# Another written order of the first and last graphs in a four-layer graph network on one core

## The chip, the core and the metric

The kernel runs on one core of a Trainium2 chip. The metric is the device time of one execution in microseconds (us). Before the change, three runs gave 2754.33, 2758.63 and 2764.74 us, so the median is 2758.63 us.

## The reference

There are 32 graphs of 512 nodes with 256 features, each with a dense 512 x 512 adjacency `adj`. Every graph goes through four layers, and every layer is `x = layernorm(x + layer(x))`, all in float32:

```python
# layer 0: GIN           h = (1 + eps) * x + adj @ x;  relu(h @ W1 + b1) @ W2 + b2
# layer 1: GAT, 4 heads  softmax over adj > 0.5 of leaky_relu(e_dst + e_src), times x @ W, plus bias
# layer 2: 8 heads       softmax(q k^T / sqrt(32) + log(adj + 1e-6)) v, then Wo and bo
# layer 3:               softmax((x W x^T) * adj, masked by node) x
```

Graphs do not depend on each other, so the work of several graphs can be interleaved freely.

## The kernel before, in words

`fast_path` first describes the work and then emits it. `prepare()` (weights, bounds) and `graph(g)` for each of the 32 graphs register steps with `plan.step`: a name, an engine, a duration that the planner assumes, the steps it comes after, the buffers it takes, and a function that emits its instructions. There are 11118 steps, 2077 of them matmul steps on PE. `Plan.run` then reads one long list, `ORDER` (a compressed text, decoded in `Plan.sequence`), and emits the steps one by one in just that order. Each engine executes its instructions in the order in which it got them, so `ORDER` is the schedule. What comes out of `Plan.run` besides is only which of several equal buffers a step takes.

```python
data = zlib.decompress(base64.b85decode(text))
...
for g, name in self.sequence(text):
    s = self.steps[g][name]
    ...
    s.emit()
```

The stock of buffers is small and sets how many graphs can be in work: 13 large ones (`B`, 128 x 2048 float32), 12 of half that size (`C`), 10 strips (`D`), 8 PSUM banks (`p`), at most 6 graphs alive.

Steps that the text below speaks of, with the graph's number ahead of the name where it matters (26i0 is step `i0` of graph 26; `P` is preparation):

- Layer 0: `la` loads the adjacency in four transfers of 256 KB with packets of 128 bytes (line 806), `lx` loads x with 512 packets of 1 KB (line 818), `at` and `atd` turn and complete it on DVE, then matmuls `h0`, `h1` (adjacency times x), `f0` to `f3`, `y0`, `y1`.
- Layer 1: `xt1`, `v10` to `v13`, then `Rt`. From `Rt` goes a round trip through DRAM that this text calls the R trip: `Rsi` stores 16 rows of 512 bytes (line 1030), `Rli` loads them back, broadcast to 128 partitions, as 1 MB (line 1037), ACT makes `z00` to `z33` of them (line 1089), DVE `zm` (line 1100), and the matmuls `o100`, `o110`, `o101`, `o111` (line 1122) use them. Then `d1`, `dt`, `yt`.
- Layer 2: `xt2`, `q`, `k`, `v2`, scores `s0` to `s7` (line 1278), exponentials on ACT (line 1291), a product on DVE (line 1300), attention `n0` to `n7` (line 1336). The softmax denominators are added up by DMAs on the POOL queue that add one SBUF buffer into another (`cd1` to `cd7` and `fd0`, `fd1`, lines 1311 and 1364). These are the sums that the change's rule speaks of: 1 MB each, packets of 8 KB. A `B` buffer that a sum reads comes free only when the sum has landed. The bias additions `xd1` to `xd3` (line 610) are DMAs of the same kind on the same queue. Then `d2` and the projections `p0`, `p1`.
- Layer 3: the result is normalised (`r30` to `r33` on ACT) and, for graphs 2 to 28, transposed by way of DRAM: `xw3i` stores it (line 695), `xl30i` to `xl33i` load it back in four transfers with packets of 128 bytes (line 708, 1024 packets each), and DVE finishes the transposition with `xe30`, `xe31` (line 727). Then the matmuls `i0`, `i1` (which need `xe3`), `t0` to `t3`, `w0` to `w3`, the last normalisation, and `out`.

SP issues all loads and stores, POOL all sums and bias additions, in the order of the list; an issue that has to wait holds up what stands behind it on the same engine. A matmul step of mode "any" runs as four 32-column parts or as one whole, according to the step before it; changing between these modes costs PE about 0.1 us.

Of the list, the middle is periodic: one graph's worth of steps of several graphs, interleaved, repeats every 83 us. Only the start (where the first graphs fill the pipe) and the end (where the last ones drain) are irregular.

Of the kernel before, what the change touches and what calls it, by code (L numbers as in the profile page):

```python
# [37 lines left out]


ORDER = (  # L40
    'c-rk;*^=bA4Fo}ux~uw{@%D}<?En8tBNL#idcEV=h<$Q|)H78&cp-6+Dx@SLCAZiUY;jy-Po=2(Kg9|4bIQx=--7b0qlKcZttiWH'
    ')UVi3wM1o+(N!sO?!@kSboLOnRjaZznpU2Y$`ZAfigFx>7Bf_=cD7N9##YpPD_$7~C|;ijj(UEXt@>3xHy;76N3rVlOPui!^;)B1'
    'Ze~6<@4HqL?@k{BpjaHe4@7HgrzkZB5`)A)G;N7_%hThlvR`h%*6Krqs$-zO7j<HsYzpl{fE;>AQ!w0m*00uTE2l8Ejf-A4WNBW2'
    '4MJq#X=SuP5JH6P#V`c+U=X@h%2q=WQG{DGQ3DOr?6X2uJYkwxL1k7$g_Vt?mKP{STpw^dE>;>3pc5T!q^Ja=mN0cfntHDR6-}+u'
    'nAw>=j45i>kgBHehK2<CjV1-9U<=_7rvXvZ8qx+z1{47&mBZEmQM3)%hf9v}c)M=zYHS5n6Q(Fnd<EK~4WKa&-#CIwtMEFK7{TzX'
    'p3qbXlF&YFUbSH)=?-kNp&5Ewbe=<S%;9PD$dqkZcJ2{<3sX+_hDA^m<M{mmmU5a0J8Z25=0@P9VJi?by7t06RU56#iy5^PaRg;h'
    'GeisdYJgaVh$S>b^Rn|)sQh6(3}7(?$T2Kf#z<w1Q#sPg0Og(pQ>8j62%3Od8l5dHDV6+i$d+EAh<`A9wm6hRkpe&jO64G2EtP(m'
    '8wZM^hA*bYmNYelfl3SEfZ3RL=!KflI2=QV)Au8+0o1~8|MI?JI_#{mE5x-C)lzpxZ*3INOQj;!LqWQviyxIEmN7<I3E^4@;u>x2'
    'Apms=TZo7c_=f?`5N~X1_Ap<AUHEbHCdE#WT{zcZ4b8!=>OdFB16mA+P1B7c=qW8PK*+wrXd)`){F0y0Tn)<-j8dL-BaX8vBk?)X'
    'CwqScyl9Mr8G&B{CkxwpY9Q=Y($P*)O&Fu9o)Muw1+a6@ezs%I5*6@1$`2J}Oy_jY*q&pz)MR#_A^xcaD<kwjnn~xvF|R63B(@BA'  # L50
    'Et*Dv$TKo#K&%ah{umasoc;>gazXn`XrGrp7ql0&S3tO+y`a6Iy<+VJ?FH=x?FH=x?FH?%Lb$B<g7$*;3J90gUeI39UeNxZLp!kj'
    'HMGp+Cb&%9NVcJW6WqT5ZK5}zwXfLzDYW*C?K3b5?Z_CX=p)}0=x1&X*{&ya?a@kkK>J5zllPHXb9|M|f%@1@42GGYR^S(TJ3vFS'
    'gm8~3GbG1kWYM%_ww6WfnK&K?nMT$$D;PgB&zZx+2NL|k%zlaT7;5IPp=eS9*mDpO+y=6PNDx{b8F>lorRJHjEX;~psI!h_xIL1f'
    'gQ8)CLn6bCTw$U0F{_xMG$v6a4=p2A3pR*>J;Nk6c_oE=HT<A*uLOmlW^2r;m(xrNE%x-SikvO`X+fSa=44x<m}$*OWoPDnWV4xO'
    'rXsXiQ=Fp=8oUK*k>jt7JCAH<&;o)H!*0BKWwJha0>vJw?MUtNvjHm6u#@6_fn*`T<D?c<ij^a@;05SOABY`46+lJ?`jKNDJ3#>o'
    'PKBPFof`6!fiw&k))n-L<dk4|O53*6w>?bAA2<{aQh2q7hf6SSf-@seA>d?-aOlBG0HdM~Z8AWC6VQTt60wdH9VY6NlH-#_8<Ip^'
    'Am;<(P<^ct`zG)Y39VQQEjrTL+8{QyWTk*okz6E1Y{%LQSwO1^q&=Vm!9?rB2K7PQ3By8L4Ky4wLO}RoqCROCtq{<Y?qosAAR7!#'
    'wV2~X2UF%G1u5h6X-;x-r0O6nJZnbU7e$$zWFc?{nkHw)P8wE5^FT2e4uhBi{)1^N5mGdQEj<k^H8Rx7@K4Mo3S-U?fMK-MHd+cV'
    '0UwKiLAf=(_hIV1lA<P$WE4V#X~_VAbC*yeSa=L1G&CD?bV&|PP@956!Hr6$PeC~~nMKe>b_Tl0=?|t4buqq?l43Pt6y2*?ix@fh'
    'UKwUi?uhD;ffOnwQ6ktTUnW%yMbeGgIs*?md58~SuW(wSl8WUuGF=$qp2Ic2O0iUXFpzZUi@GP%NFO{Zx)zNo)<_z@NLh8nuMymz'  # L60
    'uEh*$BTxs551F5tWlt*#D>(`2=}S*cks!u>xsdbKFm<cJ71L0J=`)+kNV1DL?qs!CdD2H!J^3!DcQa5Eu0c1-s^mW9e3=;VVoV!='
    '`AdbgB28-GSi?OQEa&3o!E3TX9IJu%SoTGe^e;PEI-&T{^yu%Y_3?f7KPZ0BOQWykoLHXyA<F+^8~5(=^70~^TP9p7*|s|Zn)O*~'
    '@8ZrORF?0z`rE&HndhYceOAP=36slUrg_mH|Nen?dhat?wI-W4b^}?k%Cz~J*CNLuNp(D;twV0xA$3O(srYgLUdt{<2Gazls@Ya!'
    'vW1Mx!d1so%H}hPY#Ro`722|FvhJ_bzAww$y1z&;A>H#_ggN$SHYMfdwk*s1rjxX7*-P1dh|{rcL8xOG*j&728jMsfLH%kYfyydp'
    ')mZHYO_|MC&W5q$AIA~vWrucO?+&*^l6NTQ>ePPrzAQgcwEN-a=(<z)*|cl>&GkKdG@Yi-MiomgF5O&nb8MJiK_}ya4Ae0nS}ZFt'
    'FP+P`bJ^qyVo$z5&s}ZjI&-PLF+@#PkJ>qOTUU<p_WgUEFpGTKNG!!1KFNgU=G)|ooF>-+{`JWRR2s47^yU*b_9pvLxo~t1%v@b^'
    '{n3H}yK%A>TD(Wmvbg43=j>o_Z*N|`LxqlsnWHg7Fi?U8En>AN6PlW^xh(&5$aT^=S$vJ>g8}X>4kPw~c!AkPpZYvQVO?HQCz2#$'
    'u6k|XcO1Vm-mZ+Mj$t=DjwR&m(5AcfauZvyJ8t9-xA$rFzY36e!-nOe*Pco{?Gs(jK(o8<=t8~_C|v4cwc3IN9H4$m-rIbBVzy=g'
    '2mZmfZSE3SpZS6d8lIO79<Hp`K?s#L^nf)0mfV0mjM!FL*Y)PQSV5|Voh&Nv-fwp;AXH2atHWgR3*dqE4DX|2+qn9yk{s{V!Sb!F'
    ';_+Z!mQuI2NSR?%Q&yTnt{HbS7LkrX)_t$jw`n0+Uu>!#tUO{JsF1|w!~a|dO_s3lnFgL-K*b4%io?a~&95#uU~D%~V_oHRk`U*H'  # L70
    'avjmgg^o2gZd2S*`ebofVI6S;=;2+Gyd6&^+$+4$73CU{@B9&>!z>ZJaK8gd=MKuJx|_MuK2(B=84nV0sFVuUO5GP2iA(CrpCUXT'
    'htllOoCOH(0t5_ee2{<%PLRSK&ENf8`y@D@9#uTJdNZ5WwJzTCBKPlJ`gViv-``d49+Tad%iRY7QE{Vuw{}buZiv3?#`{p=ZMnL4'
    'nnzF#-YXwwU|?_ym~PXwo6+MuSSzAIU-=LO@6d&ebW9<LU_n)-1;TYabOASSy3e?iS-gn_igllGjN(337!Lz}cu{e?Yz{D%hP)SR'
    '?m`|H_*@0b-AbV2H5;d`gZ08l;)xBfyU`=#gBI>GWP3QEcBBjgq(7dvB0;3~X~buw`tc#+&J;Hxkk@N;rKaFBh(bT$b+>P~+wJY`'
    '<6eSY??L9Zn#Tr}m)=*d;2p<0VWQvPxon3MV@h#k{P4}AY2SPj<ZVj)h(QZ@&tK^|H^-2DCeiP6JW0{sq^<V!Bfie_QrpU(m2e-;'
    'Cq&%sSHgfPQR3$isxD$y87m6TsT%kHyva4P(@V@UK{ggSpUSCYVEn<uBT@;RF$Fvx*@<7AQiyO4+`Am{^PV4nljOjEb9<pG@HPLy'
    '-Nk<+D;KoCgqFz41?>gx6%a0HFK91luULCQdqI0adqI0adqI1x5H72|puM2I0>Wjr7ql0&7qtK9(DpA>i2n)g6S#mEp9^wQe-GTh'
    '0Ik>;Xv<e@{}ftz#`XzXTExUR&Zri7Y$vvoL|+BC@{H~iy!H(37i7;jL-A!jkLH84z}M)M;+Xzp168gvE$st)Asa%G+5<17%O3hf'
    '%S%~jauXYk!Nl?Y{deThe)BH*TC4gbNqblfa{H~y{mzu#3ymgT=*Bd?%oYNi$@d}wN)wP$!2bP^$krWYyyfa0rEK@Xztp5E3#hpX'
    '6o?K%q>BtTSTuf;>D+u7QYD`_Xvg3>v~{qBnL`8#HEs4J*h?@e08+e_4xAEVy6+JYHqubHBI|hbkOa@6%rDs9nNGL&U>oXjl(eMa'  # L80
    'eTv-tug;>&0=5ei#4U)=Ose1K*=7YZ0K=bYEH2rq(rLf27Law*^8#z|GD=%poBPC3Pe=swZB=1hw<^ccigsOkDIc9Lc$<ptYcY~F'
    'KuTUIC|_}8i{R)ETO;&+DNMHGMQ%*ZN-~#PyJZ^P5gOV>#<)<gk4FR|NzQj4(R7&Dr8<Kz4!R&x<rK1h_}`n<R}hSE#WA~)uzvSH'
    '2YlBXPV9~#e2Bn%ESvWZlAP#DmLJT4<i|2B75p4H*ZqEP%>julv&fNl{Gkps^4PB{2fnVff_)ialavc+cam24_9<9r$IHCdW!uO;'
    '0Oi9S0;Hy1U7sFs$gzb(gRN25btP%rCM%$xfb1Y`3ZfGg5(I^&GQ58T&%Via-vC#zp4=|hSJjyu6mR%AmSd5!%p)M9m+)NV*f*xt'
    '%c_!3I#kX(jGEH=gcom-D-}T{JdXjvzOb*7RK_<k+IVlIkWE8^+RvY)1_15PPY>>U-L}e5-TLZ-nA>FG=ZusxO+L(Cl*AzLF_Kv5'
    'k^R>CQJKt73ZKLi7<^`c4^R{hmXE?Qx3U&!ZY}woNLhmOF^l7HxIItW+5(GPmgduTBSRAtgind{TzW0tx~pyuhD&V>Fz5&LDh$k>'
    '!-Aq3!JI_n7TzPl*1>T32T(vNnl<<gGpVcR{5SgrGPGQBVi%|3c1xFDdRZsBm?)`y;WeOu)tFwve~1W29u&BDV9UCZHkik%3$FB+'
    '7gUf<Q92aq1^Ys_G1(Wve+JbSd>}Bpx_0o>R!7=BppkfMKjE&+E5!V#n^f!hdO|*>BQ;);sBm6Cmun-56#zIIyzHWOpP=142nB-P'
    'yo0!+ZG9=OC@(RinEL-|_Fy}$n6{>%+aSg*HoM(fom-no@z621y88HTOH#hwL){)o0G08!$__5&H=ifo`fKesyS;go_RWKcuOnu#'
    '(Aqk=*MK6{z<?*AjqgVkkRQR8fn*a2quqm&#}gT=7kT5fccT&bMZbEx?LLz2=6c)Q;|bHg3@;jSbMrH6UG!Yyb;OEkt}ZYpKOnkp'  # L90
# [1991 lines left out]
```

## Time and profile before

| | |
|---|---|
| median of three runs | 2758.63 us |
| the profiled execution's own time | 2757.91 us |
| its span, first to last instruction | 2756.2 us |
| PE busy | 2699.6 us (98%) |
| DVE, ACT, POOL busy | 2162.4 (78%), 1716.5 (62%), 480.4 us (17%) |
| mean granted TensorE clock | 0.992 |
| DMA queue q0 (POOL: sums, bias additions) | 45568 packets, 277.89 MB, 53.4% of the 16 engines' time |
| DMA queue q1 (SP: loads and stores) | 429872 packets, 136.18 MB, 24.4% |
| a sum on the POOL queue, issue to landing | min 6.9, median 8.8, max 17.3 us |

The span is what the engines did; the execution's own time is 1.7 us longer. PE's busy time counts matmuls that overlap by some 0.17 us at their ends as one. "Idle before, releaser" names how long an engine stood still ahead of an instruction and whose end set it free. The granted clock is the share of full speed at which TensorE ran.

### The profile page before, as it was taken

The numbers are of one execution on the slowest core, as the hardware profiler recorded it, in microseconds if no ns is written. First come the engines' busy times: TensorE is split into PE (matmuls) and PEld (weight loads), VectorE is DVE, ScalarE is ACT, GpSimd is POOL, SyncE is SP. The second block draws the span as 40 slices with busy tenths as digits, with TensorE's granted clock in tenths as the row PEclk, the third lists the DMA queues.
The fourth block names the chain that finished last, engine by engine and source line by source line (L and its number), as shares of the span: only waits on it lengthen the run. The fifth ranks groups of instructions, "written<-read, shape, count | busy, mean of one in ns | idle before, by whom it ended". The sixth has DMA issues, their size and how long they took to land.

```text
span 2756.2 us, 68553 instructions
## 1 busy us (share of the span) xinstructions
PE 2699.6 (98%) x28884; PEld 1309.0 (47%) x28884; DVE 2162.4 (78%) x4257; ACT 1716.5 (62%) x3320; POOL 480.4 (17%) x526
## 2 busy tenths in 40 slices
PE   8999999999999999999999999999999999898998
...
GB/s 169 81 137 148 162 164 163 170 158 162 168 155 152 173 161 162 159 158 154 169 161 170 155 154 158 176 159 170 147 160 149 175 154 159 153 93 150 152 127 33
DMA packets 476739, 418.80 MB, mean 152 GB/s; under 512 B 377789, under 2 KB 431497, under 8 KB 444553
## 3 DMA queue, kind: packets, MB, share of 16 engines
q0 software_dynamic: 45568, 277.89, 53.4%
q1 hardware_dynamic: 429872, 136.18, 24.4%
...
## 4 chain that ended last, share of the span: by engine, by line
PE 81%; DMA 4%; DVE 3%; issue 1%; ACT 1%; SPq 1%; POOL 0%; DVEq 0%; POOLq 0%; ACTq 0%
PE s L1278 8%; PE o_ps L1336 7%; PE o_ps L331 7%; PE o_ps L1122 6%; PE v_ps L331 6%; PE hT_ps L331 6%; PE y_ps L327 5%; PE h1T_ps L331 4%; PE s L331 4%; PE o2p_ps L331 4%; PE s L327 3%; PE iT_ps L327 3%; DMA z<-z 2%; PE qT_ps L327 2%; PE kT_ps L331 2%; PE kT_ps L327 2%
## 5 line engine op out<-in xcount | busy, mean ns | idle before, releaser
L1300 DVE SCALAR_TENSOR_TENSOR z<-AT,z 128x1024 f32<-128x1024 f32 x512 | 609.5, 1214 | 97.6 <-ACT z L1291 97.0
L1291 ACT ACTIVATE z<-s 128x512 f32<-128x512 f32 x1024 | 540.0, 607 | 141.3 <-PE s L1278 129.8
L1089 ACT ACTIVATE z<-R_bc,nT,S 128x512 f32<-128x512 f32 x512 | 374.6, 807 | 89.6 <-DMA z<-z 77.6
L669 ACT ACTIVATE x<-x,shift,rstd 128x256 f32<-128x256 f32 x508 | 273.8, 594 | 174.1 <-DVE shift L654 164.3
L1100 DVE SCALAR_TENSOR_TENSOR z<-z,T,edge 128x512 f32<-128x512 f32 x512 | 347.7, 744 | 16.5 <-ACT z L1089 16.4
L646 POOL TENSOR_TENSOR rstd<-ve,nhalf 128x4 f32<-128x4 f32 (+1 forms) x131 | 173.2, 1371 | 897.2 <-DVE ve L640 885.7
L1311 POOL DMA_DIRECT2D z<-z x186 | 174.8, 943 | 874.4 <-PE o_ps L1336 481.8
L1278 PE MATMUL s<-qT,kT 32*128 32x512 f32 x2048 | 272.8, 626 | 6.5 <-ACT kT L1249 6.5
L1336 PE MATMUL o_ps<-z,v 128*32 128x512 f32 x2048 | 249.7, 596 | 0.0
L1524 DVE TENSOR_TENSOR z<-s,AT 128x512 f32<-128x512 f32 x128 | 88.0, 690 | 204.1 <-PE s L327 104.0
L1150 DVE TENSOR_TENSOR z<-z 128x512 f32<-128x512 f32 (+1 forms) x256 | 229.5, 950 | 6.0 <-PE o_ps L1122 5.4
L1122 PE MATMUL o_ps<-z,v 128*32 128x512 f32 x2048 | 229.4, 593 | 1.1 <-ACT z L1291 1.1
L623 DVE BATCH_NORM_STATS2 st<-x 128x6 f32<-128x256 f32 x508 | 212.8, 419 | 11.0
L331 PE MATMUL o_ps<-x,z 128*32 128x257 f32 x3744 | 214.3, 380 | 0.0
L331 PE MATMUL hT_ps<-AT,x 128*32 128x384 f32 (+2 forms) x2592 | 181.5, 383 | 0.0
L327 PE MATMUL y_ps<-w_sb,h1T 128*128 128x256 f32 x816 | 180.9, 379 | 0.0
L1278 PEld LDWEIGHTS s<-qT,kT 32*128 32x128 f32 x2048 | 96.6, 184 | 142.0 <-issue 52.8
L331 PEld LDWEIGHTS o_ps<-x,z 128*32 128x32 f32 x3744 | 120.9, 110 | 87.8 <-issue 5.7
L327 PEld LDWEIGHTS y_ps<-w_sb,h1T 128*128 128x128 f32 x816 | 152.9, 190 | 19.6
L331 PE MATMUL h1T_ps<-hT,w_sb 128*32 128x512 f32 x1312 | 147.2, 592 | 0.0
L610 POOL DMA_DIRECT2D x<-biases x96 | 107.2, 1139 | 177.5 <-issue 72.5
L1122 PEld LDWEIGHTS o_ps<-z,v 128*32 128x32 f32 x2048 | 65.3, 110 | 149.3 <-issue 125.3
...
## 6 DMA issues: line engine op xcount, KB each, us to landing
...
```

Source lines behind the costliest of these rows:

```text
L327: nc.tensor.matmul(out, lhsT, rhs, start=start, stop=stop)
L331: nc.tensor.matmul(out[part], lhsT[:, part], rhs, start=start, stop=stop)
L623: nc.vector.bn_stats(t[f"st{n}"][:, c, :], t["xo" if n == 4 else "x"][:, c, :D])
L669: nc.scalar.activation(t[into][:, c, :D] if into else xn, xn, AF.Identity, bias=t[f"shift{n}"][:, c : c + 1], scale=t[f"rstd{n}"][:, c : c ...
L1089: nc.scalar.activation(t[f"e{h}"][:, c, :], t["Rbc"][:, h, :], AF.Relu, bias=t["nT"][:, h, c : c + 1], scale=t["S"][:, h, c : c + 1],)
L1100: nc.vector.scalar_tensor_tensor(z, z, t["T"][:, h, c : c + 1], t["edge"][:, c, :], op0=ALU.add, op1=ALU.mult)
L1122: nc.tensor.matmul(po[32 * q : 32 * q + 32, :], t["v"][:, c, hp * P + 32 * q : hp * P + 32 * q + 32], t[f"e{2*hp+q//2}"][:, c, :], start=( ...
L1150: nc.vector.tensor_add(z[:, :m, :], z[:, :m, :], z[:, m : 2 * m, :])
L1278: nc.tensor.matmul(pk, t["k"][hs, o, blk(c)], t["q"][hs, o, :], start=True, stop=True)
L1291: nc.scalar.activation(t[f"E{k}"][:, j, :], t[f"ps{k}{j}"], AF.Exp, scale=QSCALE)
L1300: nc.vector.scalar_tensor_tensor(z, t["AT"][:, c, None, :].to_broadcast([P, 2, N]), ADJ_EPS, z, op0=ALU.add, op1=ALU.mult,)
L1336: nc.tensor.matmul(t[f"n{o}"][32 * j : 32 * j + 32, :], t["v2"][:, c, o * P + F2 * j : o * P + F2 * (j + 1)], t[f"E{k}"][:, j, :], start=( ...
```

## The change

Only the text `ORDER` changes. The same 11118 steps are emitted, in another order; no step is added, removed or altered, and the rule by which the order was searched is not in the kernel.

```diff
 ORDER = (
-    'c-rk;*^=bA4Fo}ux~uw{@%D}<?En8tBNL#idcEV=h<$Q|)H78&cp-6+Dx@SLCAZiUY;jy-Po=2(Kg9|4bIQx=--7b0qlKcZttiWH'
...
-    'RB#@ZF;SgQu^J<aoNJ@=9kgSg4{Lm_^w<{i`Pi}B-h__gO@8qb+3-gB4`D>{SO'
+    'c-rk;?Q-Kd4g?91)TbTW$;@PD=N{wU|IrTJAZ6!j?`o^|*WF4pacqeq!NwOAw3(70B9h`5Z)6-P9ar)={2flDjB{w@=TwDnRW;5@'
...
+    'I{M^0IXch0omW)*h0#1~mLZ0sY5YP<H0|U2TOZFy^6~r<B}mE4*ehD5_;|>SJ`%6<6Hizkt+mS&O>^?On5mkd&}bDee#P5o74O^p'
 )
```

Decoded, the two lists compare so. Of the 2077 matmul steps, the places 7 to 386 and 1661 to 2056 differ; the 1274 between (from the middle of graph 6 to graph 25; 508 to 2167 us in the profile of before) and the last 21 are the same. The changes of matmul mode fall from 497 to 487.

As an example, matmul steps (PE) and the issues on POOL between 26p1, the last matmul before the DRAM transposition of graph 26, and 26i0, the first matmul after it:

```text
before  PE    26p1 27s6 27n3 27n4 28y1 27n5 27s7 29h0 29h1 27n6 29f0 28xt10 28xt11 29f1 28v10
              28v11 28v12 28v13 29f2 28Rt 29f3 26i0
        POOL  27cd1 27cd3 26dev3 27cd5 27cd2 28dev1 25dev4 27cd7 27fd0 27cd6 29xd1
after   PE    26p1 29h0 29h1 27n1 27s7 28xt10 28xt11 29f0 27n2 27n3 28v10 28v11 29f1 29f2 29f3
              27n4 27n5 27n6 28v12 28v13 26i0
        POOL  28dev1 27cd1 27xd3 26dev3 29xd1 27cd3 27cd5 25dev4 27cd7 27cd2
```

Only the order on one engine binds; how PE's list and POOL's interlock is settled by what each issue waits for. A sum `cd` of an odd number k waits for `n` of k - 1 and for its own product, 29xd1 for 29h1, and each waits for the issue ahead of it on POOL.

At more places the matmul steps between two dependent ones change: between 29Rt and 31h0 there stand more (31h0 moves back, behind 29o100 and 27w3), between `Rt` and `o100` of graphs 0, 1, 2, 5, 28 and 29 fewer, and graph 28's `p1` and `i0` stand closer together. At the start, SP issues the four adjacency strips of graph 0 ahead of its x (before: x second), ACT issues `eps` first (before: the two attention vectors first), and PE transposes two weights between 0h1 and 0f0 (before: behind 0y1).

More of the change, by code (lines that the diff above doesn't have):

```diff
@@ L40 @@
 ORDER = (
-    'c-rk;*^=bA4Fo}ux~uw{@%D}<?En8tBNL#idcEV=h<$Q|)H78&cp-6+Dx@SLCAZiUY;jy-Po=2(Kg9|4bIQx=--7b0qlKcZttiWH'
[L42 to L90, printed above, removed]
@@ L91 @@
-    'n<FvLQ_NyhFb!iO^C-55W%=OJjy!B{TZ1>8kM@*!FC%%~Twl1vMnYRIRtjl!2l;sC(xP}1>cSVFvUZso$Wq<{`DA3)c^qqYKB*ed'
-    'RB#@ZF;SgQu^J<aoNJ@=9kgSg4{Lm_^w<{i`Pi}B-h__gO@8qb+3-gB4`D>{SO'
+    'c-rk;?Q-Kd4g?91)TbTW$;@PD=N{wU|IrTJAZ6!j?`o^|*WF4pacqeq!NwOAw3(70B9h`5Z)6-P9ar)={2flDjB{w@=TwDnRW;5@'
+    'I{M^0IXch0omW)*h0#1~mLZ0sY5YP<H0|U2TOZFy^6~r<B}mE4*ehD5_;|>SJ`%6<6Hizkt+mS&O>^?On5mkd&}bDee#P5o74O^p'
+    't@K-XSb84nV?lHcab*k{f_mrvOE_B%H2ik9^mcxe-z~fpqU9mo@y<`@=S;d}Uk=UD?qznPGt~hRKjRa%rrCT@ybYmL<8Ft|q3B}+'
@@ new lines @@
+    ')B!KVPlAaO00+!<V*U>Y;OE)s3W%jXFvjZFVz?mz0885O#6@<hx!^4z=WQ{yJ_F*GfoLkF_>W7*-c|Ect45>EkO<g^4sefAK2yGf'
+    'blE67%*(74D%wJi_}DFpst7R)XHGK-$Wxq5CCryfGDv`~N`{n&!qF5~>F0<Kf%6#vF24XY0?K0010glcx~NOjk&Y%r*xR|TC^hC#'
+    ')Fm!4IvT}1{PgoKpS1NOYg{SS4<CX8WcIB27|Jwy$pK9$o`>J;GWq{Fkw-IyxCI)-%|3r#$IPtI=KMrKw=QfzUNEqq2DUCrC@UcG'
+    '+iUd~tHlauiVrDOqkfITS3m79>?<o<peZdRRmf<Z&*-6s^h)EvJvmTE=NPPDYM4Z&{E)#aO^JZ;IsoGpG~~_dw^~SBsNldIO(0vL'
+    'Sp8~kU24v<Qu(;Mls?6-v+UO@nl&BQE7VY|`5A56{389>r>VpuRK@nC)#s?;?2xlHVp8zhAhkzT({5cbdKyzWc0uq9!%2nb(KbIV'
@@ new lines @@
+    '%INZ0EnJ-dg$8JP^kw!%Z>CkGBcK=~tBJ%<sDn|?fA!%?mOfVE4<n_*VS9ALWlszecH{Pqn~@_TYBOq}A2gRfO_LJAPD8`~(!&Nr'
+    'c42~x3}x069AipHDMj9MhsF7Dk%-NVVt#``E@Qg$dtAP7u92SznuXVl$QN?<Xc#?0cqCaw&=f(<U(z$p@odkrkTH;g<VY#JUk{fJ'
+    '+52QTq6|f*NE7zjK7xw&U|>x6jL$s?#PzQ!K6>gsSj4by7d@to<iWH@K*~7!8l?LZjA1NG`a%HO&V3FBG)6mSn3wE)1j=;4sRLGK'
+    'i?Os3A{&7*Rv>>LXk$%wLVH4c280vZ6WSBnGuEEap3t7qp3t7qp3t5vgwtwIXisR*fN)yv3GE5(3GM#{v;*7!3@z)y9bA;Ba<5IX'
+    '%fABdpMbWbH=wnz*#053_KNK*FdbS-6@{*YvT>lFI(oVDBLZD}_L82^{yVa{SH_}3g<otZWCoZR46}o(QAX2X2#`^M@|nLA6!=jq'
@@ new lines @@
+    'mOP4I0bEoTL;Tb!3sEZT`~f+t+L`o}!#+ko2OlBS8pVDV)M;r{JETh5Z8}BY!3pRHf!d)@vrApMW1=15Ue)a7#EkA@m?2{_dlvWL'
+    'y(o<))&MPAFSlo)4Ke}d$?`w6<3I*Mr4t6oh@c3lEhdi5i>x?$bIu?|y}y^zQ>e51T0y54%offUWDpeKS(o>-ysbztifX3{q%m=t'
+    'Qc5Lw5<XjU6LM5_2fe`90JYCf;bCwI0~BJ0d*mRn1h7y@uTzI%_G)XlK@@s3eTc*y$uA%ibMSOVft0Qq9S6I`N^mer@L)&)i3)#w'
+    'BBS9@Z}&6_3J2o^&ye9GEa^TC_T`}1l1h1Ta`XYWW>5&=j8v2iKOel6;9um<x9UuuP9Q0n^a~yIo?=DI*FY4ZPSeXt&|`AgebBz>'
+    'ivf(KPE*29N%(hIeGe2t5Fuin3V}WjGD#2x>`4g8Un3PP04CX$<bx>L5-H39nTs&Me-ID`QHcl``8zJ64EBw6a#Z2)k{G<YlLJ;p'
@@ new lines @@
+    '0yG8Z<cm(i=5nWe1Y0LiJZ?W?bq^VxffX8!5XL*{etA&Af>e=)e<330&?KobrQ0H74|y*xTrkr@JxcBn9Vd7Q^mjrTG^&(4E2<-^'
+    'B=n>RQ-Wdg)8~e-fRiIyWJE~XJ7NoI1feQ=9|i>^?ifWVLWBoc2kA>0kqfDT&_z-}Ba)*67McYx50k)IG#ETB(_u%4sYEOczJm-x'
+    'T<52yejCS=h*^285sdr`0Y8c1BQ(=PPbAmT+?c2}=VvlVM;_^sf6$;boTf9yUb0(I$hxAfCray!7+4?qSuvsLF%rj+Aq>AmL0e6<'
+    '{oug`4Tie45t$FJ%%Sr965d9-3-aD^VTc?dK5J*Gj0IGzih^24^ADPob~=+jL-x^=4#Jnl4Rk~Xbz|VBUTuVc%nvY?{OpPl4Az@H'
+    '*BVE>u-BnSk|Y`KxJt=;-g;@uoTt5~m-9Vu*~sACAoV%TU@S40ihk)<dm7iTr(ci3f_vVe9gH9`9qiMCP3vj9Rv$=etq$Q&kSRS0'
@@ new lines @@
+    '*gxMVYjGX%DjiMTFt=C-B7aEU{D=<odc9r~d|Fy-T!afO>o+6{4F2QCAl8nf_@(b6x7)|ZubX?Ucdzdb%Iy|DNZOTyURUt$^hSb|'
+    '++<ns>c^WbSO2toC~;Z1O!lZdUuMMW#uUZ5E}QIou9NLd8<5b&n3l~gqrUm%uRh=k2}-lVRUoNYP(p3V9`F?RARoYIRpcNf>oiS~'
+    'loM7!VnG6yAOWXozwdL((<WE%b)5=uxk|cbHUV3-T>KfTs!S8Iw@t*&k5#s&KCx}n_Yc)&vAnd~_3cfsdXY<>$wbtA{k&dt{w^;2'
+    'yz25slUiMvHp}M9+GJA_@pP8^{qB+18i;jz^`_oAt@#~j*BlQj0_WQv2%2|O$N6T-5nudRvn;m8+E%1GaQ>TC;i_^Ccwe*M-e%+s'
+    '+E10#S~b9>_ga3q%>2ty+4VR52}Yo?n{1yR;g-dJy!VICVqcg#Xhzj$ru#I*pet#%TpRfca4W^lVF447F+lW5_lB)`Ygt!WxrTOo'
```

26 lines of the change are left out of this document (added).

## Prediction

> **What bounds the kernel now.** First the busy shares and the slices, then the middle by stretches of 500 us. In the fences below, PE is busy 98% of the span, and from 500 to 2000 us it has no idle time (499.06, 499.89 and 500.00 of 500 us): the periodic middle is bound by PE's own work, which the change does not touch. The slices show where PE is not full: the first, and the last six.
>
> ```profile
> PE 2699.6 (98%) x28884; PEld 1309.0 (47%) x28884; DVE 2162.4 (78%) x4257; ACT 1716.5 (62%) x3320; POOL 480.4 (17%) x526
> PE   8999999999999999999999999999999999898998
> ```
>
> ```profile
> 500.00:1000.00 500.00, 499.06 (x5512) 241.97 (x5513) 409.69 (x798) 320.94 (x624) 89.60 (x96) 1.00 0.83 161
> 1000.00:1500.00 500.00, 499.89 (x5530) 241.04 (x5532) 409.17 (x795) 321.33 (x623) 89.57 (x96) 1.00 0.85 161
> 1500.00:2000.00 500.00, 500.00 (x5532) 242.19 (x5528) 409.25 (x799) 320.07 (x619) 90.55 (x97) 1.00 0.83 161
> ```
>
> Next PE's waits, from 0 to 420 us and from 2170 us to the end (total, times, longest). Few are large.
>
> ```profile
> PE AT_t L838 <- DMA A<-in_adj_dram: 7.8, 2, 5.7
> PE s L1278 <- ACT kT L1249: 6.5, 1, 6.5
> PE hT_ps L327 <- DVE ATd L844: 2.2, 1, 2.2
> ```
>
> ```profile
> PE iT_ps L327 <- DVE xT L727: 13.3, 2, 12.9
> PE hT_ps L331 <- DVE z L1100: 5.9, 1, 5.9
> PE ok_ps L1603 <- DVE okr L1601: 3.3, 1, 3.3
> ```
>
> PE's timeline places them and shows that each costs more than its idle time, since the matmuls behind it run longer than elsewhere:
>
> ```profile
> 182.96 2.09 PE L1278 MATMUL s<-qT,kT 32*128 32x512 f32 x8 [6.46 <-ACT kT L1249]
> 190.47 1.14 PE L1278 MATMUL s<-qT,kT 32*128 32x512 f32 x8
> ...
> 2293.77 3.67 PE L327 MATMUL iT_ps<-xT,w_sb 128*128 128x512 f32 x8 [0.38 <-DVE xT L727]
> 2382.96 5.73 PE L327 MATMUL iT_ps<-xT,w_sb 128*128 128x512 f32 x8 [12.93 <-DVE xT L727]
> 2497.97 0.66 PE L331 MATMUL hT_ps<-ATd,x 128*32 128x128 f32 x8 [5.92 <-DVE z L1100]
> ```
>
> I took the start-to-start time of every one of the 2077 matmul steps and compared it with the median of its kind (h 3.46, y 3.45, f, q, k, i, t and o1 1.72, w 1.74, p 1.73, s 0.96, v and n 0.86 to 0.89, xt 0.44, yt 0.22, a change of mode about 0.1). The excess is 19.6 us in the part of the list that changes at the start and 34.4 us in the part at the end. Three places hold 33.1 of these 54: 1s0 at 183 us (6.46 idle and 2.8 of slow matmuls, 9.3), 26i0 at 2383 (12.93 and 2.3, 15.2), 31h0 at 2498 (5.92 and 2.7, 8.6). The first fill of PE is 4.8; some 16 lie in waits below 2 us.
>
> Why 26i0 waited: the chain of waits there has `2348.82 12.68 DMA x_dram<-x` and `2370.78 11.29 DMA xL<-x_dram`, so the DRAM transposition was late. The DMA view tells what held it. From 2371 to 2377 us sums ran, and the SP queue (q1) moved 0.02 MB; from 2202 to 2214, without a sum, it moved 1.33 MB in 10013 packets.
>
> ```profile
> q0 software_dynamic: 199, 1.21, 100.2%
> q1 hardware_dynamic: 142, 0.02, 3.8%
> ```
>
> ```profile
> q1 hardware_dynamic: 10013, 1.33, 90.1%
> ```
>
> So 128-byte packets all but stop while a sum runs. At 31h0 the chain has `2483.07 14.76 DMA x<-in_x_dram`: a load of 1 KB packets, beside a bias addition. At 1s0 it was another thing: ACT stood still until a sum had freed the buffer of 2z30, and the q and k copies stood behind that on ACT.
>
> **The change part by part.** PE's work stays. With the medians above, the new order of the first 385 matmul steps costs 482.6 us instead of 482.9 and that of the last 417 costs 540.0 instead of 539.7; ten changes of mode less save nothing, as other changes take their place. So only waits count. I measure a place by its cover: the matmul work that the list puts between a step and the step that depends on it by way of other engines. If what lies between needs longer than the cover, PE waits.
>
> 26i0. From the end of 26p1 the cover falls from 27.4 to 24.7 us. Need in the profile: 6.6 us to 26xw3i, then 33.4 to 26xe30, then 0.8. The 33.4 held four sums, two half ones and a bias addition. In other graphs this leg took 15.2 (graph 2, one sum), 18.8 (graph 3, one) and 21.8 (graph 25, three); the middle has at most 22.2. In the new order the POOL issues can start 3.5 us before the end of 26p1 (27cd1, 27xd3) and 6.9 (29xd1), 12.5 (27cd3) and 21.2 us (27cd5) after it, where the old one had two at 2.7 and four at 15.9. That is two sums in the leg, so between 18.8 and 21.8: a need of 26 to 29 and a wait of 1.5 to 4.6. I take 3.5; bounds 0 (15.2) and 7.4 (22.2, with 2.5 for slow matmuls).
>
> 31h0. Its x is issued behind 29's R trip. Cover from 29Rt: 17.8 before, 27.3 after; the need was 24. No wait; bounds 0 and 3.
>
> 1s0. 2z30 now takes the buffer that 0cd2 frees, three sums earlier than 0cd6, which freed it before. That wait goes. What is late next is graph 2's R trip, with its 16 z steps of 0.81 us on ACT ahead of graph 1's q and k copies: the cover from 2Rt to 2o100 falls from 27.3 to 19.1 us. Need before 27.4: 7.1 to Rli, 12.8 to the first z, 7.5 to the zm. But of the 7.1 most was 4la3, which SP issued between Rsi and Rli, and which the new order puts behind; the middle's trips take 3.1, 8.7 and 10.8, other graphs' last leg 5.3 to 7.5. So 17 to 20, and for 1s0 some 31 against 29.5: I take 2, bounds 0 and 11 (27.4 less 19.1, and 2.7 slow).
>
> 29o100. Cover 26.8 to 23.8, need 25.1 before, with four sums about it instead of three: 2, bounds 0 and 5.
>
> Graphs 0, 1, 5 have covers of 20.8, 20.7 and 21.2 for needs of 24.0, 22.3 and 21.3 that include ACT's own order: 1 together, bounds 0 and 5. Graph 28's cover falls from 33.1 to 22.6; its need was 47, with SP held for 15.1 us ahead of Rsi by 30la3 and 30lx, which now stand ahead of 26xw3i. I take 0, bound 25.
>
> Close reuse of PSUM banks: 27s3 and 27v21 take banks that ACT empties right after 27s2 and 27s3, 0.6 us each; a few such: 2, bounds 0 and 6.
>
> Start: `eps` lands earlier, x later; both are ahead of 0h0, which waited 2.2 us for ATd. 0, bounds -1.5 and 1.5.
>
> Unlisted waits: the order of before lost 33 us at three places that no wait of its middle foretells. For the new one I add half of the mean of those three, 5.5; bounds 0 and 22 (two of them).
>
> Sum: -33.1 + 3.5 + 2 + 2 + 1 + 2 + 5.5 = -17.1. From the execution's own 2757.9 us that is 2740.8; I say **2740**. The median of the runs, 2758.6, is 0.03% above it.
>
> A rule that speaks against this: the Trainium skill, "TensorE: Matmul & The Clock Gate", section "What's actually happening", says that TensorE drops to half its clock after about 3.4 us of idling and needs about as long a busy stretch to return. The granted clock here agrees: 0.63 from 176 to 190 us, 0.66 from 2368 to 2388, no loss behind 2.24 us of idling. By that rule, as an estimate, the 3.5 us at 26i0 would cost 1.7 more if they come in one piece, so 2742.
>
> **Rivals.** (a) The waits go and others of like size come: the covers are shorter in six places, and the bounds of graph 2 (11), 26i0 (7) and 29o100 (5) together would give 2757.9 - 33.1 + 23 + 4 = 2752, within 0.5%. For it: 24.7 is less than any leg from p1 to i0 took (31 at the least). Against: those longer legs waited for DVE, not for the DMA. Chance 0.31; it includes the case that sums hit 26's transposition as hard as before (2757).
>
> (b) Slower: the R trip, the one chain whose cover shrinks nearly everywhere, needs as long as in the same graphs before. Deficits 3.2 (0), 1.6 (1), 8.3 (2), 24.8 (28), 1.3 (29), together 39, with 5.4 for slow matmuls behind two of them, 5 at 26i0 and 3 at other places: 2757.9 - 33.1 + 52 = 2777. It is decided at graph 28: only if SP is held there again by some 15 us is the sum positive. Against it: 30la3 and 30lx no longer stand ahead of 28Rsi. Chance 0.11.
>
> (c) The forecast, 2726 to 2745: 0.58.
>
> **Numbers.** More than 0.5% is what a measurement of this kernel can tell from no change. Faster (below 2745) 0.58, within 0.5% (to 2772) 0.31, slower 0.11. The range is 2726 (no unlisted wait, the others near their low ends) to 2764, which takes in most of (a).
>
> **What would show it.** Right: 26i0 with less than 5 us of idle time; no wait at 1s0 and 31h0; the middle unchanged; no idle of more than 5 us anywhere past 20 us. Wrong: a PE wait of 6 us or more at an o_ps L1122 (R trip) or iT_ps, a clock below 0.9 in a stretch that had 1.00, or a middle that is no longer full.

## The result, and the profile after

The changed kernel takes 2754.93 us (median of 18 runs, 2741.65 to 2758.47), the kernel before on the same chip 2759.89 (18 runs, 2753.82 to 2766.54). The ratio is 0.9979, with a 95% interval of 0.9970 to 0.9988. So the change saves 0.2%, 5 us, where 17 were forecast: within 0.5%, and 15 us above the predicted time.

The profiled execution does not show this. It took 2744.93 us, 13.0 less than the profiled one of before. It is one of three short ones (2741.7, 2744.9, 2746.5); the other 15 runs took 2750.9 to 2758.5. The page of the changed kernel (busy times; PE by slices) and its answer for a stretch of the middle look as before:

```profile
PE 2698.5 (98%) x28728; PEld 1311.6 (48%) x28728; DVE 2164.0 (79%) x4257; ACT 1712.8 (62%) x3320; POOL 477.9 (17%) x526
PE   8999999999999999999999999999999999899998
```

```profile
500.00:1000.00 500.00, 500.00 (x5552) 242.63 (x5548) 408.37 (x795) 321.65 (x626) 89.15 (x96) 1.00 0.84 161
```

The middle is full, as it was. The three waits that were to go are gone or small: none at 1s0, 0.3 us at 31h1, and at 26i0 2.04 us of idle time where there were 12.93. What PE waits for from 2170 us to the end is now this (total, times, longest; lines are two higher than in before):

```profile
PE o_ps L1124 <- DVE z L1102: 6.6, 3, 5.5
...
PE qT_ps L329 <- ACT xT L1232: 2.6, 1, 2.6
PE iT_ps L333 <- DVE xT L729: 2.0, 1, 2.0
PE o_ps L333 <- ACT z L1532: 1.8, 2, 1.1
PE y_ps L333 <- ACT h1T L925: 1.4, 2, 0.8
```

One large wait and four small ones stand where two large ones were. PE's timeline places the first and the third:

```profile
2362.55 4.42 PE L333 MATMUL iT_ps<-xT,w_sb 128*32 128x512 f32 x24 [2.04 <-DVE xT L729]
...
2396.99 3.62 PE L1124 MATMUL o_ps<-z,v 128*32 128x512 f32 x12 [5.53 <-DVE z L1102]
```

The second is 28o100, the end of graph 28's R trip, with 2.2 us of slow matmuls behind it (the granted clock is 0.77 from 2389 to 2404 us): 7.8 us at a place that the prediction had costed at nothing. Its sign of being right, no idle time of more than 5 us past 20 us, fails here by 0.5; its sign of being wrong, a wait of 6 us or more at a matmul of the R trip, shows in the first repeat below (7.7).

From here on I measure three stretches on PE: the **head** ends where place 386 of the matmul list starts, the last one that differs ahead of the common middle (5s5 in before, 5n3 in the changed order), the **tail** runs from the end of the middle to the end of the last `w`. In before the entry is at 508.4 us and the tail takes 576.6; in the changed kernel's first profile 497.6 and 574.1. So even in a lucky execution 10.9 us came from the head and 2.5 from the tail, which was to give some 12 (23.8 for its two waits, less 3.5, 2 and 2 and most of the unlisted 5.5).

### The profile page after: what moved, and what is told of

It is laid out like the page before. It is cut to its first block, busy times and chain, and to the rows that moved or that the text cites. A ratio compares the mean times of both kernels' runs of the same rounds, so it can differ in the third digit from the quotient of the medians.

```text
span 2743.0 us, 68241 instructions
## 1 busy us (share of the span) xinstructions
PE 2698.5 (98%) x28728; PEld 1311.6 (48%) x28728; DVE 2164.0 (79%) x4257; ACT 1712.8 (62%) x3320; POOL 477.9 (17%) x526
## 5 line engine op out<-in xcount | busy, mean ns | idle before, releaser
L1102 DVE SCALAR_TENSOR_TENSOR z<-z,T,edge 128x512 f32<-128x512 f32 x512 | 347.4, 744 | 18.4 <-ACT z L1091 18.2
L625 DVE BATCH_NORM_STATS2 st<-x 128x6 f32<-128x256 f32 x508 | 213.0, 419 | 10.9
L333 PE MATMUL hT_ps<-AT,x 128*32 128x384 f32 (+2 forms) x2496 | 172.8, 379 | 0.0
L333 PE MATMUL h1T_ps<-hT,w_sb 128*32 128x512 f32 x1392 | 155.8, 592 | 0.0
## 6 DMA issues: line engine op xcount, KB each, us to landing
x<-biases POOLq DMA_DIRECT2D x96, 512.0 KB, 10.1
```

The lines of the kernel that those rows point to most:

```text
L333: nc.tensor.matmul(out[part], lhsT[:, part], rhs, start=start, stop=stop)
L625: nc.vector.bn_stats(t[f"st{n}"][:, c, :], t["xo" if n == 4 else "x"][:, c, :D])
L1102: nc.vector.scalar_tensor_tensor(z, z, t["T"][:, h, c : c + 1], t["edge"][:, c, :], op0=ALU.add, op1=ALU.mult)
```

## The experiments

All medians stand beside a run of the kernel before on the same chip (2757.8 to 2760.3 us).

### One half of the change at a time

```diff
 head_after
-list of before, steps 1 to 4400 of 11118
+list of after, steps 1 to 4400; then the list of before
 tail_after
-list of before, steps 4401 to 11118
+list of before, steps 1 to 4400; then the list of after
```

> The first graphs in the changed order, the last graphs in the old one; the middle is common to both orders, so the list is cut there. Theory 1 (the gain is made in the first graphs and given back in the last ones): the first graphs are worth 10.6 to 10.9 us by the two profiled runs, so the median falls from 2759.9 to about 2749, below the changed kernel's 2754.9. Rival (the changed order is worth its 5 us evenly, or its profiled run was merely a lucky one in the first graphs): no lower than 2755. In the trace, both: the first matmul of the middle's common part comes at about 497.5 us (old 508.4), and the old order's two waits at the end (12.9 and 5.9 us, for the transposed x of graph 26 and for the first layer of graph 31) come back.

> The first graphs in the old order, the last graphs in the changed one. Theory 1: the changed tail is worth nothing or costs up to 6 us in a usual run, so the median is 2758 to 2766. Rival (evenly shared gain): 2757.5. A third, that the forecast's sum is right for the tail (-33.1+9.3 for the two waits, and some 6 of new ones, about -15 us): 2745. In the trace: the step into the middle at 508 us, no wait for the x of graph 31, and one of 5 to 8 us at the transposed sum of graph 28's weights (the R trip), which the forecast had at zero.

Measured: the new head alone 2752.33 us (ratio 0.9973, 0.9964 to 0.9982), the new tail alone 2762.82 us (1.0012, 1.0003 to 1.0022). The differences of -7.9 and +2.6 us add up to the change's -5. So the whole gain is the head's, and the tail, rid of 24 us in two waits, is no shorter at all: it took 578.7 us in the profile of the new tail alone, and the old tail 574.0 in that of the new head alone. As expected, the old waits came back with the old tail (26i0, 31h0), and the new one stood at 28o100 in the other (7.2 us). Theory 1 holds as to where the gain is made. Its size for the head (10.6 to 10.9 us) was missed, and so was the entry into the middle, expected at 497.5 us: in the profile of the new head alone it lies at 504.2, since the score step 5s0 waited 6.9 us there. The last experiments are about that wait.

### The changed kernel twice more, unchanged

> The changed kernel once more, unchanged, for its trace: the first trace was of a run of 2744.9 us, 10 us below the median of 18. Theory 1 (one of the last graphs' steps races small packets against a sum, and the race ends differently from run to run): a run near 2755 shows one or two waits in the last graphs that the first trace lacks, of 4 to 10 us together with a stretch of half clock, and the first graphs as before (the middle entered at 497 to 498 us). Rival (the first trace was lucky in the first graphs): the middle is entered 5 to 10 us later. Second rival (clock alone): the same waits and longer steps.

> As the run before it, for a second trace: Theory 1 expects the same entry into the middle and another sum of waits in the last graphs; the rivals as there.

Measured: 2750.45 and 2753.28 us. Both theories are partly right. The tail does change a little (28o100 waits 7.7 and 5.2 us), but the tails take 575.1 and 573.8 us; what differs is the entry into the middle, 501.6 and 505.2 us against 497.6. So the first profile was lucky in the **head**, which Theory 1 did not expect. Two things do it. In the second repeat, graph 5's R trip is late. SyncE's timeline and ScalarE's there:

```profile
408.30 0.33 SPq L1032 DMA_DIRECT2D R_dram<-R_rows  x1
...
413.16 0.34 SPq L1039 DMA_DIRECT2D R_bc<-R_dram  x1
```

```profile
426.78 2.94 ACT L1091 ACTIVATE z<-R_bc,nT,S 128x512 f32<-128x512 f32 x4 [10.39 <-DMA R_bc<-R_dram]
```

The write of 16 small rows needed 4.9 us, and the broadcast load behind it was issued at 413.2, after two sums (411.6 and 413.1); z could start at 426.8. In the first profile the write needed 2.2 us, the load went out at 408.1, ahead of the sums (409.3 and 410.7), and z started 5.8 us later. The second thing is the clock. PE's timeline at graph 5's scores, in the first profile and in the first repeat:

```profile
470.58 2.00 PE L1280 MATMUL s<-qT,kT 32*128 32x512 f32 x16 [2.39 <-ACT qT L1251]
```

```profile
473.07 2.69 PE L1280 MATMUL s<-qT,kT 32*128 32x512 f32 x16 [2.50 <-ACT qT L1251]
```

The same wait, but behind the second the granted clock from 473 to 477 us is 0.66, behind the first 1.00, and the next steps took 1.5 us longer. Of the 4.0 us by which this repeat enters the middle later, another 1.3 arise in the same way behind 2xt21.

### The sums without their data

In both lists each sum is still issued and waited for, but moves 32 of 2048 columns (186 sums `cd` of 1 MB each, and 62 `fd`, which take 64 partitions and so half of that); the softmax denominators of the second layer are then incomplete.

```diff
-                nc.gpsimd.dma_start(dst, src, accum_op=ALU.add)
+                nc.gpsimd.dma_start(dst[:, :32], src[:, :32], accum_op=ALU.add)
...
-                    nc.gpsimd.dma_start(z[dst], z[src], accum_op=ALU.add)
+                    nc.gpsimd.dma_start(z[dst][:, :32], z[src][:, :32], accum_op=ALU.add)
```

> The old order, with the sums of the second layer's z left out but for 32 of 2048 columns (each is still issued, waited for and frees its buffers; the denominators are then incomplete). Theory 1 (the waits that differ between the two orders are collisions of loads with these sums): the 9.3 us at graph 1, the 15.2 us at the transposed x of graph 26 and the 8.6 us at graph 31 go, and nothing comes in their place: 2760 - 33 = 2727, if the x load of graph 31 is counted too, 2736 if it is late for its buffer and not for the sums. Rival (they are waits in the order of VectorE and ScalarE): within 5 us of 2760. The common middle stays as it was in both.

> The changed order with the same edit (the denominators are incomplete). Theory 1: the 7.8 us at graph 28's R trip, the 3.9 us at graph 26's transposed x and what the head owes to the sums go, 12 to 16 us: 2740 to 2743; the 2.3 to 2.8 us waits at graphs 27, 30 and 31 stay if they are of the order of ScalarE and VectorE. So without the sums the old order would be the shorter one, by 5 to 15 us. Rival (order of the engines): within 4 us of 2755, and the changed order stays the shorter.

Measured: 2716.47 us (0.9850, 0.9835 to 0.9864) and 2716.32 us (0.9847, 0.9833 to 0.9861). **The two orders are equally long without the sums' data**, and the sums cost the old one 41 us and the changed one 39 (against the medians of their runs; 41 and 36 by the ratios). This is more than either theory said, and the old order is not the shorter one, as Theory 1 had it. It also settles where the four small waits of the tail come from, which I had put down to the order of ScalarE and VectorE: they are gone as well. All that PE waits for from 2150 to 2640 us, changed order:

```profile
PE xT_t L1228 <- DVE y L1197: 0.5, 1, 0.5
PE y_t L1191 <- DVE rd L1184: 0.2, 1, 0.2
```

The tails take 547.4 and 548.2 us, 26 to 29 less; the four runs of the second lie within 3.3 us, against 17 of the changed kernel, so the spread comes with the sums too. Whether a sum costs by slowing a load beside it or by freeing a buffer late, these two runs do not separate; the traces below show both.

### Graph 28's R trip

The timeline of the changed kernel, SyncE first, then POOL's sums, then ScalarE:

```profile
2369.30 0.34 SPq L1032 DMA_DIRECT2D R_dram<-R_rows  x1
2375.04 0.35 SPq L1039 DMA_DIRECT2D R_bc<-R_dram  x1
...
2364.59 1.79 POOL L1313 DMA_DIRECT2D z<-z  x2
2372.21 0.85 POOL L1313 DMA_DIRECT2D z<-z  x1 [5.83 <-DMA z<-z]
...
2390.50 3.63 ACT L1091 ACTIVATE z<-R_bc,nT,S 128x512 f32<-128x512 f32 x5 [12.02 <-DMA R_bc<-R_dram]
```

SyncE is not held any more (0.3 us after Rt). But the write lands 5.7 us later, and the load needs 15.5 us till the first z. From 2376 to 2388 us the two queues moved:

```profile
q0 software_dynamic: 237, 1.59, 76.5%
q1 hardware_dynamic: 136, 1.05, 25.5%
```

(Packets, MB, share.) The 1.05 MB of q1 is R's load, in packets of 8 KB as the sums' are. Two kernels test it: one starts the trip earlier, the other takes the data from graph 27's sums only (its denominators are then incomplete).

```diff
 r28_early, PE
+28Rt
 26i0 26i1 27n7
-28Rt
 26t0
 light27
-                nc.gpsimd.dma_start(dst, src, accum_op=ALU.add)
+                n = 32 if g == 27 else 4 * N; nc.gpsimd.dma_start(dst[:, :n], src[:, :n], accum_op=ALU.add)
```

> The changed order with one step moved on TensorE: graph 28's first step of the R trip (the transposition that starts it) ahead of the transposed x of graph 26 and one step of graph 27, 6 us earlier. Theory 1 (the trip is 5 to 8 us longer than the work that covers it, since its load runs beside two sums): the wait before graph 28's first sum falls from 5.2 to 7.7 us to at most 2, and the median by 5 to 8 us, to 2747 to 2750. Rival (the sums end the trip, whenever it starts: the load then shares with one more sum): the first sum waits as long as before and the median stays at 2755.

> The changed order with the sums of graph 27 alone cut to 32 of 2048 columns (its denominators are then incomplete); all other sums are whole. Theory 1: the wait before graph 28's first sum of 7 to 10 us and the 3 to 4 us at graph 26's transposed x go, since the loads that they wait for run beside graph 27's sums and no other; the waits of graphs 27, 30 and 31 (their loads run beside the sums of graphs 26 and 28) stay. 10 to 13 us below the changed kernel, 2742 to 2745. Rival (the waits move on to the next step): 2750 or more.

Measured: 2743.01 us (0.9955, 0.9941 to 0.9968) and 2742.34 us (0.9941, 0.9924 to 0.9957). Against the changed kernel's ratio that is 0.24% and 0.38%, 7 and 10 us; by the medians 12 and 13. The trips, from the end of 28Rt:

| | to Rsi | to Rli | to first z | to zm00, zm10 | together | wait and slow matmuls at 28o100 |
|---|---|---|---|---|---|---|
| before | 15.1 | 7.4 | 7.1 | 17.8 | 47.4 | none |
| after (three profiles) | 0.3 | 5.7 to 6.0 | 14.3 to 15.5 | 8.4 to 11.4 | 29.6 to 32.1 | 7.2 to 10.0 |
| trip begun earlier | 1.4 | 1.5 | 13.0 | 12.4 | 28.3 | below 0.7 |
| graph 27's sums without data | 0.3 | 1.5 | 7.7 | 10.8 | 20.3 | none |

With the sums the load takes 5 to 8 us more, and in the changed kernel the write 4; without them the trip is shorter than its cover of 22.6. The stretch from 2330 to 2420 us (length, PE busy first) in the changed kernel, with the trip begun earlier, and with light sums of graph 27:

```profile
2330.00:2420.00 90.00, 82.44 (x829) 42.57 (x822) 56.34 (x116) 39.15 (x75) 16.07 (x17) 0.94 0.77 146
```

```profile
2330.00:2420.00 90.00, 86.90 (x1134) 42.58 (x1123) 63.26 (x135) 41.88 (x79) 16.10 (x17) 1.00 0.79 149
```

```profile
2330.00:2420.00 90.00, 90.00 (x942) 47.53 (x927) 66.80 (x143) 44.69 (x85) 16.03 (x17) 1.00 0.40 76
```

The tails take 568.1 and 559.6 us, against 573.8 to 575.1. So the wait is real, the sums of one graph make it, and 6 to 7 us of it can be had by one step's place. The rival (the trip moves and waits as long) falls. The 3.1 us that the second row still lacks are a new wait: 28Rt, now earlier, stands that long for its input from ScalarE, while 26i0 and 28o100 hardly wait any more. With the light sums of graph 27 the wait at 31y1, which was expected to stay, went as well.

### The small waits: ScalarE held by a late load

ScalarE's timeline in the changed kernel shows what stands ahead of the small ones. It holds still at the first z of a graph, until a sum frees a buffer or R has landed:

```profile
225.77 1.52 ACT L1091 ACTIVATE z<-R_bc,nT,S 128x512 f32<-128x512 f32 x2 [7.41 <-DMA z<-z]
...
2477.29 1.52 ACT L1091 ACTIVATE z<-R_bc,nT,S 128x512 f32<-128x512 f32 x2 [5.80 <-DMA R_bc<-R_dram]
2512.60 0.81 ACT L1091 ACTIVATE z<-R_bc,nT,S 128x512 f32<-128x512 f32 x1 [7.92 <-DMA R_bc<-R_dram]
2576.25 0.81 ACT L1091 ACTIVATE z<-R_bc,nT,S 128x512 f32<-128x512 f32 x1 [3.98 <-DMA R_bc<-R_dram]
```

Queued behind it are evictions (copies of matmul results out of PSUM) that have nothing to do with R, and PE waits for those: 2xt21, 27w1, 31y1, 30q0. The views of PE's waits name ScalarE for them, and so they look like a matter of its order.

```diff
 ACT
-3z10 3z11 2r22 2r23
+2r22 2r23 3z10 3z11
-29z00 29z01 27te1 29z02 27te2 27te3
+27te1 27te2 27te3 29z00 29z01 29z02
-30z00 31fe0 30z10 30z20 30z11 31fe1 31fe2 30z30 31fe3
+31fe0 31fe1 31fe2 31fe3 30z00 30z10 30z20 30z11 30z30
-31z00 30r23 31z01 31z02 31z10 31z03 31z11 28te0 30xe21 30xe20
+30r23 31z00 31z01 31z02 30xe21 30xe20 31z10 31z03 31z11 28te0
```

> As r28_early, and on ScalarE four groups of z activations (the first ones of graphs 3, 29, 30 and 31, which stand still until a sum frees their buffer or until the R load lands) are put behind the few evictions that were queued behind them (of graphs 2, 27, 31 and 30). Theory 1, second form (a late load or sum that a covering step count misses because it holds ScalarE, and TensorE then waits for the evictions queued there): the waits of 2.5 to 3.2 us before graph 2's transposition, in graph 27's output rows, in graph 31's second step and at graph 30's q, and the half clock after some of them, go: 10 to 14 us less than r28_early, 2729 to 2733. Rival (the time goes to the transfers, so a wait taken away here comes back at the next step that needs one): 2739 to 2745, as r28_early.

> The changed order with the ScalarE edit alone; graph 28's R trip starts where the change put it. If the two edits are independent: 12 us above the run with both, and 10 to 14 below the changed kernel, 2741 to 2745. Rival: 2751 to 2757.

Measured: 2742.54 us (0.9937, 0.9918 to 0.9956; runs from 2732.3 to 2750.0) and 2747.23 us (0.9960, 0.9946 to 0.9973). All four waits are gone from both traces, and yet the first is where r28_early was. Two reasons: in the tail 28w0 and 28w1, which need graph 28's te evictions that moved back, now lose 6.9 and 6.8 us with the slow matmuls (the tails are 569.3 and 573.2 us, 1 more and 1 less than without the edit); and in the profile of the first the wait at 5s0 is 6.9 us. So for the tail the rival is right: what is taken away here is paid at the next step. The second lies between its two expectations and gains 5 us by the ratios; by its one profile the tail gives 1 of them, so most should be the head's.

### Graph 5's two races

```diff
 ACT
-5ve13 4e33 2te1 2te2 5R
+5ve13 5R 4e33 2te1 2te2
 PE
-4q1 4v22 4v23 5Rt
+4q1 5Rt 4v22 4v23
```

r28_r5 has this and 28Rt earlier; r28_r5_act has besides the ScalarE edits of graphs 3, 29 and 30 and, of the last one, 30r23 ahead of 31z00.

> r28_early with the same for graph 5: the step that starts its R trip stands two steps (1.7 us) earlier on TensorE, its input 1.6 us earlier on ScalarE. In the runs so far graph 5's R either lands 8 us after its load is issued (write landed in 2.2 us, load issued ahead of two sums) or 18 us after it (write landed in 4.9 us, load behind the sums), and TensorE's entry into the middle goes with it. Theory 1: the early case becomes the rule, the entry lies at 496 to 500 us, the median 2 to 4 us below r28_early (2739 to 2741) and the spread of the runs, 11.7 us, falls below 8. Rival (the race moves along with the step): median and spread as r28_early.

> The run before it, with those of the ScalarE edits whose waits did not come back when tried (graphs 3, 29 and 30; of graph 31's only the last normalisation of graph 30 ahead of the first z). Theory 1: the waits before graph 2's transposition, in graph 27's output rows and in graph 31's second step are gone (8 us with the half clock behind the first), that at graph 30's q is shorter, and the median lies 5 to 9 us below the run before it, 2731 to 2735. Rival (waits come back): the same as the run before it.

Measured: 2745.15 us (0.9945, 0.9929 to 0.9961; 2737.7 to 2750.3) and 2743.33 us (0.9936, 0.9920 to 0.9952; 2736.4 to 2748.1). A miss for both expectations; the numbers are the rivals'. Graph 5's R is early in both profiles, but the entry lies at 506.3 and 505.3 us, since 6.7 and 6.8 us are lost at 5s0 instead. SyncE's and ScalarE's timelines of the first show a second race:

```profile
466.98 1.49 SPq L1583 DMA_DIRECT2D out_dram<-x  x1
...
476.81 0.59 ACT L1251 COPY qT<-qT_ps 128x512 f32<-128x512 f32 x1 [8.76 <-DMA out_dram<-x]
```

5q is evicted into the buffer out of which graph 2's result is stored, and the store is issued just ahead of a sum, here by 0.74 us (467.72). It landed 9.8 us later. Other profiles of kernels with this order show the edge: with leads of 0.74 us (light sums of graph 27), 0.75 (the first repeat), 0.87 (the first profile) and 1.20 (r28_early) it landed in 4.5 to 5.1 us; with leads of 0.66 (the new head alone), 0.66 (act_r28), 0.74 (r28_r5) and 0.75 (r28_r5_act) in 9.8 to 10.1. At three quarters of a microsecond it goes either way. By the end of the store's issue on SyncE the two groups part: it comes 0.15 to 0.63 us after the sum's issue in the four quick ones and 0.75 to 0.91 us in the four slow ones; whether that is cause or effect no run shows. In the second repeat and in act_only the store was issued 0.4 and 0.6 us behind a sum and took 9.6 and 9.8 us; 5q came late there, and PE had no wait at 5s0. So the store is moved, in the changed kernel alone and with the other edits:

```diff
 SP
-7la1 7la2 7la3 2out0
+2out0 7la1 7la2 7la3
```

> The changed order with one step moved on SyncE's queue: the store of graph 2's output is issued ahead of the last three loads of graph 7's adjacency and not behind them (11 us earlier). Theory 1 (what differs from run to run in the first graphs is a race at graph 5: the store frees the buffer that graph 5's q is evicted into, and lands 4.5 us after its issue where it leads a sum's issue by 0.9 us, 9.8 us where it leads by 0.7): no wait for that store on ScalarE, no wait over 1 us before graph 5's scores, entry into the middle at 493 to 498 us unless graph 5's R load loses its own race, median 3 to 6 us below the changed kernel, 2749 to 2752. Rival (the wait moves to the next step that a sum holds): 2753 to 2757.

> The changed order with all edits that removed their wait when tried: graph 28's and graph 5's R trips begun earlier, the ScalarE edits at graphs 3, 29, 30 and the one step of graph 30, and the store of graph 2's output ahead of the loads. Theory 1: as the run with the two R trips and the ScalarE edits (2743), less the 6.8 us before graph 5's scores and the half clock behind it: 2733 to 2737. Rival: 2741 to 2745.

Measured: 2747.81 us (0.9958, 0.9944 to 0.9972; runs within 5.5 us) and **2733.44 us (0.9904, 0.9889 to 0.9920; runs within 5.0 us)**. In the first, the store goes out 11 us earlier and ScalarE's wait is only PE's own q:

```profile
456.37 0.38 SPq L1583 DMA_DIRECT2D out_dram<-x  x1
...
468.90 0.59 ACT L1251 COPY qT<-qT_ps 128x512 f32<-128x512 f32 x1 [1.18 <-PE qT_ps L329]
```

No wait at 5s0; the entry is at 497.3 us, although 0h1 and 4d1 were at least as slow as in the repeats. In the second the entry is at 492.5 us and the tail takes 568.6. It differs from r28_r5_act (2743.33 us, 0.9936) in the place of this one store, and its median lies where Theory 1 expected it. So the head's gains had been there and one race hid them; the last kernel beats both, by 1.0% and 0.8%. Its page:

```profile
PE 2698.6 (99%) x28992; PEld 1309.0 (48%) x28992; DVE 2163.1 (79%) x4257; ACT 1714.6 (63%) x3320; POOL 478.0 (17%) x526
```

## Why the prediction was wrong, step by step

The times are those of the changed kernel's three profiles.

| step | forecast | measured |
|---|---|---|
| 1s0, 26i0 and 31h0 as they were | -33.1 | gone |
| 26i0 by its new cover | 3.5 (0 to 7.4) | 3.9 in the first: 2.04 idle, the rest slow matmuls |
| 31h0 | 0 | 0.3 (at 31h1) |
| graph 2's R trip | 2 (0 to 11) | 0; trip 18.2, cover 19.1 |
| 29o100 | 2 (0 to 5) | no wait there; the same late load held ScalarE (27w1, 2.4) |
| graphs 0, 1, 5 | 1 (0 to 5) | graph 5: 2.5 at 5s0, or 7.1 at 5o110, 5o101, 5o111 |
| **graph 28's R trip** | **0** (0 to 25) | **7.2 to 10.0** |
| PSUM banks | 2 (0 to 6) | about 1 (27v21) |
| unlisted waits | 5.5 (0 to 22) | some 16: 2xt21 3.0, 27o101 2.3, 27w1 2.4, 28d2 2.2, 31y1 2.0, 30q0 2.8, 4d1 1.4 |

The mechanism that removes the three waits was right, and so were the two covers worked out anew, 26i0 (a need of 26.7 us, forecast 26 to 29) and 31h0. At 31h0 the company was misread: the late x was not beside a bias addition (the last one was issued at 2471.04 us, 12 us ahead of the load) but beside two sums, issued at 2479.10 and 2485.36, and the wait is gone with light sums. **The step that failed is "Graph 28's cover falls from 33.1 to 22.6 ... I take 0".** The reason given, that SP would no longer be held, came true; but the prediction's own legs spoke against the value. 47.4 less the 15.1 of the hold is 32.3, still 9.7 above the cover, and the wait turned out at 7 to 10. I had in effect put in the trip of the middle, 22.6 us, which runs beside other sums. With graph 27's sums in the way the load alone took 14.3 to 15.5 us to the first z, against 8.7 in the middle.

The second term that was mis-sized is the unlisted waits, 5.5 against some 16. I had measured cover only along the R trip to its own matmul, o100. A late R shows as well in what is queued behind the first z on ScalarE, a chain that no cover of mine contained. That the rule of one cover per chain misses this is shown for the four places (the waits go when the z are put behind the evictions); that the tail then does not get shorter is shown too. In the other direction a term was missing. Against its run without the sums' data the old order's profile is 41.5 us longer, and only 33 of these stood at the three places; the changed order's first profile is 29.0 longer. So some 8 us of smaller waits went with the old order as well, which accounts for a profile 13 us shorter although the table's new waits come to 31.

Of the rivals, (a) came nearest: waits of like size, 2752 against a measured 2754.9. But its reason was not the one measured: graph 2 and 29o100, two of its three places, did not wait. (b) named the right place, graph 28, and the wrong cause: SP was not held there. For the forecast's 15 us of error, the trip of graph 28 accounts for about 7 (by the ratios, begun earlier), and the kernel without that one wait stands at 2743 on its own chip, or at 2747 to 2748 by its ratio, 3 to 8 us above the forecast. The rest I can't split exactly: it holds the tail's small waits, which can't be had one by one, and graph 5's store, which costs some 6 us (by the ratio of out2_early, 0.21%).

The clock deserves a word, as the prediction had weighed the rule of the Trainium skill ("TensorE: Matmul & The Clock Gate", section "What's actually happening"): half clock after about 3.4 us of idling, in windows that run on regardless of the program. The runs show the windows: in each of the 16 profiles all stretches of half clock (65 in total) start on one grid of 3.413 us, to within 4 ns, and all but the last of a profile are 3.41, 6.83, 10.24 or 13.65 us long. They disagree with the figure. 2.39 us of idling at 5s0 left the clock at 1.00, 2.50 brought 0.66 behind it; and at 2xt21 2.30 us left 1.00 in one run and 2.02 gave 0.88 (226 to 240 us) in another. What counts is how much of the idling falls into one window: the end of a window splits the 2.39 us into 0.96 and 1.43, and 2.24 of the 2.50 us lie in one. Past the first 20 us, each of the 45 windows at full clock in which PE idled for 2.06 us or more was followed by half clock, and none with less than 1.44; between these it went either way. So shorter waits than the page says can cost, and the same wait costs in one run and not in the next.

In two of the profiles, of the new tail alone and of the store moved alone, the middle took 3 to 6 us more (1663 to 1664 us from entry to exit, against 1658 to 1660 in the others). The traces place this at its end: ScalarE stood 3.3 and 1.7 us at 24e60, an exponential of graph 24, until a sum had landed, PE's 25yt2 waited 3.1 and 1.6 us behind it, and half clock followed. What stays open is why that sum was late in just these two, and whether another order of the tail's sums could have its 26 us; no run changed POOL's order.
